# Products of an all-zero stationary operand added at five places of a four-layer attention kernel

## The chip, the cores and the metric

The program runs on 1 core of one Trainium2 chip. The metric is the device time of one execution in microseconds (us), lower is better. Before the change three executions took 2467.56, 2470.31 and 2482.42 us; the median is 2470.31 us.

## What is computed

An activation `x` of 2 x 1024 tokens with 288 features passes through four layers. The context has 2 x 154 rows of 288 features, and there are 16 heads of 18 features each.

Layers L0 and L1 have the same form. The quantised linear layer rounds activations and weights to 8-bit integers with scales of their own:

```python
h = layer_norm(x, ln1_g, ln1_b, 1e-06)
q8, s, sm = quant_act(h)
q, k, v = (quant_linear(q8, s, sm, w, b) for w, b in ((wq1, bq1), (wk1, bk1), (wv1, bv1)))
a = attn(q, k, v)                                   # self-attention, 1024 keys
x = x + quant_linear(*quant_act(a), wo1, bo1)
h = layer_norm(x, ln2_g, ln2_b, 1e-05)
q = quant_linear(*quant_act(h), wq2, bq2)
a = attn(q, cond @ wk2.T + bk2, cond @ wv2.T + bv2, mask)   # cross-attention, 154 keys
x = x + quant_linear(*quant_act(a), wo2, bo2)
h = quant_linear(*quant_act(layer_norm(x, ln3_g, ln3_b, 1e-05)), wfc1, bfc1)   # 1152 wide
x = x + quant_linear(*quant_act(gelu(h)), wfc2, bfc2)
```

Layers L2 and L3 are plain: `x` is projected to queries, attends in two separate softmaxes to the first 86 and to the last 68 context rows, and two output projections are added to `x`.

## The kernel before

Tokens lie on the 128 partitions; four blocks of 128 tokens make one row tile of 512. The code writes out a program order by hand, as Python generators that are advanced in turn (`beside`), and the framework then orders the instructions of each engine at build time on a timeline of its own (`schedule_with_timeline_sim=True`), taking what is ready and comes first in program order. On the chip each engine runs its own list in that order.

**Main stream.** `self_attention` makes 32 steps (2 layers x 2 batch elements x 4 head groups x 2 halves of the queries), `run` (L869) drives them. A step has `pre` (fetches by DMA on SP's queue), `maxima` of the next step (`self_maxima`: 32 products at L600 and 32 reductions on VectorE at L607, then `store_maxima`: parts on GpSimd, four transposes at L575, a copy on ScalarE at L581 and DMAs on ScalarE's queue at L585 into rows 108 to 119 of the next step's query tile), and `products` (`attend`, L695): for each of 8 key tiles four products of keys and queries (`weights_unit`, L660) with an Exp on ScalarE (L662), and, one key tile later, `weigh` (L701), which adds the four heads' weighted values into one PSUM tile `po` of pool `ps_o`, which has one buffer. The last `weigh` of a step (m = 7) is in `end`, which `run` calls after the first unit of the next step; `heads_back` then reads `po`.

**Side stream.** Beside the main stream run the weights' preparation (`prep_*`), the projections for the next self-attention (`SelfAttention.prepare`), and for each layer and batch element `cross_attention` (L1175) and `feed_forward` (L1312). In `cross_attention` the values of the context come from `context_values` (L1167, products at L456) once `wv` has been loaded on GpSimd's queue; `transpose_mask` (L1228) copies the last mask columns on ScalarE (L1232) and transposes eight blocks on TensorE (L1238). In `feed_forward`, `linear` (L1324) makes a 1152-wide row block with 12 products, `gelu` (L1336) runs two Gelu activations back to back on ScalarE (L1338, L1339), `integers` quantises, `output` transposes (L1354) and multiplies (L1360).

**Plain layers.** Layers L2 and L3 run as 8 blocks of 4 steps. `attend_pairs` (L822) makes eight key-query products a step (L660, Exp at L662), and `weigh` (L832) twice a step weighs two heads by two key spans into a new `po` of pool `ps_o` (L674), which VectorE transposes out (L847). `out` (L1494) makes the output projection.

PSUM tiles of the side stream, of the transposes and of the projections come from `mm` (L145), pool `ps_m` with two buffers used in turn. `zero16` of the change is the stationary operand, `ident16` the 128x128 identity in bf16 that is there already.

Of the kernel before, what the change touches and what calls it, by code (L numbers as in the profile page):

```python
# [11 lines left out]
BF16 = mybir.dt.bfloat16  # L12
# [4 lines left out]
P = 128  # L17
# [36 lines left out]
def tile_xattn(ctx: ExitStack, tc: tile.TileContext, ins: dict, out: bass.AP):  # L54
    nc = tc.nc
# [3 lines left out]
    const = ctx.enter_context(tc.tile_pool(name="const", bufs=1))  # L59
# [16 lines left out]
    nc.vector.memset(neghalf, -0.5)  # L76
    nmagic = const.tile([P, 1], F32, name="nmagic")
    nc.vector.memset(nmagic, -MAGIC)

# [66 lines left out]
    def mm(name, dtype=F32):  # L148
        n = 512 if dtype == F32 else 1024
        return ps_m.tile([P, n], dtype, tag="mm", name=name)  # L150
# [517 lines left out]
    def strips(po, pairs, start, stop):  # L668


        last = None
        for i in reversed(range(4)):
            lhsT, rhs = pairs[i]
            made = nc.tensor.matmul(  # L674
                po[32 * i : 32 * i + 32, :], lhsT=lhsT, rhs=rhs, start=start, stop=stop
            )
            if last is not None:
                follow(made, last)
            last = made
# [15 lines left out]
    def attend(qt, g, key_tiles, a, name):  # L695


        po = ps_o.tile([P, HQ], F32, tag="o", name=f"{name}o")
        made = {}

        def weigh(m):  # L701
            es, v = made.pop(m)
            strips(
                po,
                [(columns(v, 4 * g + j), es[j]) for j in range(4)],
                m == 0,
                m == len(key_tiles) - 1,
            )

        def step(m, half):  # L710
            keys, v = key_tiles[m]
            if half == 0:
                if m - 1 in made:
                    weigh(m - 1)
                made[m] = [], v
            for j in (2 * half, 2 * half + 1):
                made[m][0].append(weights_unit(qt, j, keys, P, f"{name}s"))

        def end():
            weigh(len(key_tiles) - 1)  # L720
            ptv, rec = heads_back(po, f"{name}o")
            av = a().rearrange("p c (g i d) -> p c g i d", g=G, i=4)
            nc.vector.tensor_tensor(
                av[:, :, g, :, :],
                ptv[:, :, :, 0:D],
                rec.unsqueeze(3).to_broadcast([P, HC, 4, D]),
                ALU.mult,
            )

        todo = [  # L730
            lambda m=m, half=half: step(m, half)
            for m in range(len(key_tiles))
            for half in range(2)
        ]
        return todo, end
# [86 lines left out]
    def attend_pairs(qt, g, keys, vs, features, name):  # L822

        made = {}

        def exps(j, n):
            k0, k1 = ((0, NTXT), (NTXT, T))[n]
            made[j, n] = weights_unit(
                qt, j, lambda j: keys(j)[:, k0:k1], k1 - k0, f"{name}s"
            )  # L830

        def weigh(j0):  # L832
            h0 = 4 * g + j0
            po = ps_o.tile([P, HQ], F32, tag="o", name=f"{name}o")
            strips(
                po,
                [
                    (columns(vs[n], h0 + j), made.pop((j0 + j, n)))
                    for j in range(2)
                    for n in range(2)  # L840
                ],
                True,
                True,
            )

            t = row512(f"{name}T")
            nc.vector.transpose(t, po)  # L847
            tv = t.rearrange("p (b e) -> p b e", e=32)
            rec = small.tile([P, HQ // 32, 1], F32, tag="rec", name=f"{name}rec")
            nc.vector.reciprocal(rec, tv[:, :, D : D + 1])  # L850
            features.add(tv, rec)

        def step(j0, n, j):
            if (j0, n, j) == (2, 0, 1):
                weigh(0)
            exps(j0 + j, n)

        todo = [
            lambda j0=j0, n=n, j=j: step(j0, n, j)
            for j0 in (0, 2)  # L860
            for n in range(2)
            for j in range(2)
        ]
        return todo, lambda: weigh(2)

    def nothing():
# [308 lines left out]
    def cross_attention(w, b, name):  # L1175
# [10 lines left out]
        wv = load_f32(bpool, w["pre"] + "wv2", 1)  # L1186
        v = bpool.tile([P, VW], F32, tag="v", name=f"{name}v")
        nc.gpsimd.memset(v, 1.0)
        context_values(v, P, b * T, wv, w["bv"], f"{name}cv")

        nr = T - P
# [36 lines left out]
        def transpose_mask(hf):  # L1228
            maskTs[hf] = bpool.tile([P, 2, HQ], F32, tag="maskT", name=f"{name}mT")

            others = view(row512(f"{name}mo"), c=HC, j=4, k=32)
            nc.scalar.copy(  # L1232
                others, masks[hf][:, :, P:TP].unsqueeze(2).to_broadcast([P, HC, 4, 32])
            )
            for kc in range(2):
                pt = mm(f"{name}mp")
                for c in range(HC):
                    nc.tensor.transpose(  # L1238
                        pt[:, c * P : (c + 1) * P],
                        others[:, c].rearrange("p j k -> p (j k)")  # L1240
                        if kc
                        else masks[hf][:, c, 0:P],
                        ident,
                    )
                nc.scalar.copy(maskTs[hf][:, kc, :], pt)
# [66 lines left out]
    def feed_forward(w, b, name):  # L1312

        qw2, row2 = w["2"]
        for hf in range(2):
            c0 = b * 8 + hf * HC
            s1 = small.tile([P, HC], F32, tag="st", name=f"{name}st")
            q = ln_quantise(c0, w["ln"], 1e-5, s1, f"{name}l")
            yield 8
            qT = transposed(q, f"{name}t")  # L1320
            yield 2
            hs, gs = {}, {}

            def linear(c):  # L1324
                hs[c] = big(f"{name}h")
                for j, wj in enumerate(w["1"]):
                    quant_linear(
                        qT,
                        c,
                        wj,  # L1330
                        s1[:, c : c + 1],
                        hs[c][:, j * C : (j + 1) * C],
                        f"{name}f",
                    )

            def gelu(c):  # L1336

                a = nc.scalar.activation(hs[c + 1], hs[c + 1], AF.Gelu)  # L1338
                follow(nc.scalar.activation(hs[c], hs[c], AF.Gelu), a)  # L1339

            def integers(c):
                s = small.tile([P, HC], F32, tag="s", name=f"{name}s")[:, 0:1]
                g = bf(f"{name}g")[:, 0:FZ]
                nc.gpsimd.memset(g[:, FF + NZ : FZ], 0.0)
                quantise(hs[c].unsqueeze(1), g.unsqueeze(1), s, 1, FF, f"{name}qs")
                gs[c] = g, s

            def output(c):
                g, s = gs[c]
                gT = view(bf(f"{name}gT")[:KF, 0 : 10 * P], k=10, t=P)  # L1350
                for k0 in (0, 5):
                    ptv = view(mm(f"{name}pt", BF16)[:KF, 0 : 5 * P], k=5, t=P)
                    for k in range(5):
                        nc.tensor.transpose(  # L1354
                            ptv[:, k, :], g[:, (k0 + k) * KF : (k0 + k + 1) * KF], ident16
                        )
                    nc.scalar.copy(gT[:, k0 : k0 + 5, :], ptv)  # L1357
                ps = mm(f"{name}o")[:, 0:C]
                for k in range(10):
                    nc.tensor.matmul(  # L1360
                        ps,
                        lhsT=gT[:, k, :],
                        rhs=qw2[:, k, :],
                        start=(k == 0),
                        stop=(k == 9),
                    )
                t = tmp(f"{name}u")
                nc.vector.scalar_tensor_tensor(t, ps, s, row2, ALU.mult, ALU.mult)
                add_to_x(c0 + c, t)


            for f, c in (
                (linear, 0),
                (linear, 1),
                (gelu, 0),
                (integers, 0),
                (linear, 2),
                (output, 0),
                (integers, 1),
                (linear, 3),  # L1380
                (gelu, 2),
                (output, 1),
                (integers, 2),
                (integers, 3),
                (output, 2),
                (output, 3),
            ):
                f(c)
                if f is not gelu:
                    yield 2  # L1390
# [357 lines left out]
```

## Time and profile before

| | |
|---|---|
| three runs, us | 2467.56, 2470.31, 2482.42 |
| span of the profiled execution, us | 2474.0 (a time of that execution beside its span is not given) |
| PE, matmuls | 1950.8 us busy, 79%, 10524 instructions |
| DVE | 1772.7 us, 72% |
| ACT | 1476.1 us, 60% |
| POOL | 972.2 us, 39% |
| mean granted TensorE clock | 0.866 of full speed |
| L660 128x512 products, self-attention | 1024, mean 409 ns |
| L674 weighing, self-attention | 2048 instructions (two for each f32 product), mean 660 ns |
| L1338 Gelu table load, Gelu | 16 of each line, 1283 and 1163 ns |

PE is TensorE's matmuls and transposes, PEld its weight loads, DVE VectorE, ACT ScalarE, POOL GpSimd, SP the engine that issues most DMAs. PEclk is the clock that TensorE was granted. Matmuls overlap in the pipeline, so the duration of one is longer than the distance between two. Idle time in brackets stands ahead of an instruction, with what ended it.

### The profile page before, as it was taken

To read this page: it belongs to the slowest core of one execution; us is meant where nothing else is said; L and a number is where in the kernel's file an instruction comes from. 1 tells how busy PE (TensorE), PEld (TensorE's weight loads), DVE (VectorE), ACT (ScalarE), POOL (GpSimd) and SP (SyncE) were. 2 spreads that over 40 slices of the span, in tenths; PEclk is the share of its full clock that TensorE was granted. 3 is DMA by queue.
4 is the path that set the end of the run, shared out by engine and by line. 5 is a ranking of instruction groups with operands and counts; after the bars stand their busy time and mean duration, and the time that the engine had idled before them with its cause. 6 is when DMAs were issued, how large, how long until landed. Compare 5 with 4: busy or idle time off the path is not lost. (4 is left out here: it accounts for less than half of the span.)

```text
span 2474.0 us, 33572 instructions
## 1 busy us (share of the span) xinstructions
PE 1950.8 (79%) x10524; PEld 847.7 (34%) x10524; DVE 1772.7 (72%) x4213; ACT 1476.1 (60%) x2897; POOL 972.2 (39%) x2038
## 2 busy tenths in 40 slices
PE   2579988788776878887679668887778886788887
PEld 1223333332233243323333233333334343443443
DVE  6699987699775658997559848893345686656665
ACT  3257767676477667756766257756646564554443
POOL 4334224651325455532353545523157462423210
PEclk9689999899787979998889589986877888889998
DMA  3523212221001322110032031100122311212221
GB/s 75 168 66 100 68 35 69 70 64 33 13 7 47 113 71 64 44 29 14 6 100 85 23 86 43 46 9 12 31 76 87 89 48 28 55 51 81 81 66 37
DMA packets 160003, 141.58 MB, mean 57 GB/s; under 512 B 44123, under 2 KB 156339, under 8 KB 159760
## 3 DMA queue, kind: packets, MB, share of 16 engines
q1 hardware_dynamic: 148656, 121.90, 17.0%
q0 software_dynamic: 3584, 12.04, 2.0%
q10 hardware_dynamic: 7584, 5.47, 1.2%
q8 instruction: 84, 1.38, 0.2%
q14 instruction: 95, 0.78, 0.1%
HBM read 96.60 MB, written 39.37 MB: 55 GB/s over the span
## 5 line engine op out<-in xcount | busy, mean ns | idle before, releaser
L662 ACT ACTIVATE L_xattn_aatse<-L_xattn_aats 128x512 f32<-128x512 f32 x1024 | 576.3, 597 | 277.1 <-PE L_xattn_aats L660 267.2
L607 DVE TENSOR_REDUCE L_xattn_amxh<-L_xattn_amx 128x1 f32<-128x512 f32 x1024 | 658.4, 679 | 74.5 <-PE L_xattn_amx L600 71.9
L660 PE MATMUL L_xattn_aats<-L_xattn_aqT,kT 120*128 120x512 bf16 x1024 | 392.2, 409 | 88.0 <-ACT L_xattn_aatse L662 46.2
L600 PE MATMUL L_xattn_amx<-kT,L_xattn_aqT 108*128 108x512 bf16 x1024 | 387.9, 414 | 65.1 <-DVE L_xattn_amxh L607 39.5
L674 PE MATMUL L_xattn_aato<-L_xattn_aatse,L_xattn_av 128*32 128x512 f32 x2048 | 300.9, 660 | 43.7 <-ACT L_xattn_aatse L662 40.6
L641 POOL TENSOR_TENSOR L_xattn_bmxm<-L_xattn_bmxm,L_xattn_bm 128x308 f32<-128x308 f32 x256 | 200.0, 787 | 158.4 <-ACT L_xattn_bmxm L640 150.4
L660 PEld LDWEIGHTS <-kT 120*128 120x128 bf16 x1024 | 96.7, 101 | 336.2 <-issue 298.7
L662 ACT ACTIVATE L_xattn_atse<-L_xattn_ats 86x512 f32<-86x512 f32 (+1 forms) x256 | 142.7, 590 | 95.0 <-PE L_xattn_ats L660 82.2
L600 PEld LDWEIGHTS <-L_xattn_aqT 108*128 108x128 bf16 x1024 | 102.7, 103 | 216.7 <-issue 162.5
L646 DVE TENSOR_REDUCE L_xattn_mxn<-L_xattn_mx 128x2 f32<-128x172 f32 (+1 forms) x512 | 124.8, 303 | 30.7 <-PE L_xattn_mx L630 27.4
L640 ACT COPY L_xattn_bmxm<-L_xattn_bmx 128x308 f32<-128x308 f32 x256 | 104.1, 417 | 67.9 <-PE L_xattn_bmx L630 23.7
L646 DVE TENSOR_REDUCE L_xattn_bmxn<-L_xattn_bmxm 128x2 f32<-128x308 f32 x256 | 116.8, 461 | 30.6 <-POOL L_xattn_bmxm L641 30.3
L660 PE MATMUL L_xattn_ats<-L_xattn_qT,L_xattn_kT 120*86 120x512 bf16 (+1 forms) x256 | 99.7, 422 | 40.8 <-DMA L_xattn_qT<-L_xattn_mxsr 18.6
L746 DVE TENSOR_TENSOR L_xattn_batse<-L_xattn_bats,L_xattn_bmT 128x512 f32<-128x512 f32 x160 | 107.5, 680 | 25.7 <-PE L_xattn_bats L752 7.5
L747 ACT ACTIVATE L_xattn_batse<-L_xattn_batse 128x512 f32<-128x512 f32 x160 | 100.3, 631 | 40.6 <-DVE L_xattn_batse L746 36.4
L1494 PE MATMUL L_xattn_o<-wo,L_xattn_p 128*128 128x288 f32 x320 | 99.9, 451 | 5.5 <-DVE L_xattn_p L819 4.6
L674 PEld LDWEIGHTS L_xattn_aato<-L_xattn_aatse,L_xattn_av 128*32 128x32 f32 x2048 | 42.2, 112 | 173.2 <-ACT L_xattn_aatse L662 144.1
L847 DVE STREAM_TRANSPOSE L_xattn_atT<-L_xattn_ato 128x512 f32<-128x512 f32 x64 | 45.6, 713 | 61.6 <-PE L_xattn_ato L674 50.1
L630 PE MATMUL L_xattn_mx<-L_xattn_kT,L_xattn_qT 108*128 108x154 bf16 x512 | 68.9, 250 | 24.1 <-DMA L_xattn_qT<-L_xattn_r 10.4
L630 PE MATMUL L_xattn_bmx<-L_xattn_bkT,L_xattn_bqT 108*128 108x154 bf16 x512 | 72.0, 244 | 16.1 <-ACT L_xattn_bmxm L640 7.1
L1360 PE MATMUL L_xattn_co<-L_xattn_wfc2t,L_xattn_cgT 117*128 117x288 bf16 x320 | 62.4, 346 | 23.4 <-ACT L_xattn_cgT L1357 22.4
L674 PE MATMUL L_xattn_ato<-L_xattn_atse,L_xattn_v 68*32 68x512 f32 (+1 forms) x512 | 74.9, 649 | 6.7 <-ACT L_xattn_atse L662 5.8
(632 smaller groups left out, 3782.0 us busy)
## 6 DMA issues: line engine op xcount, KB each, us to landing
kT<-L_xattn_akr SPq DMA_DIRECT2D x192, 72.0 KB
L_xattn_aqT<-L_xattn_aqr SPq DMA_DIRECT2D x192, 72.0 KB
L_xattn_bqT<-L_xattn_bqr SPq DMA_DIRECT2D x192, 72.0 KB
L_xattn_qT<-L_xattn_r SPq DMA_DIRECT2D x192, 72.0 KB
L_xattn_akr<-L_xattn_akst SPq DMA_DIRECT2D x16, 324.0 KB
L_xattn_aqr<-L_xattn_aqst SPq DMA_DIRECT2D x16, 324.0 KB
L_xattn_bqr<-L_xattn_bqst SPq DMA_DIRECT2D x16, 324.0 KB
L_xattn_r<-L_xattn_qst SPq DMA_DIRECT2D x16, 324.0 KB
```

The source lines that it names most:

```text
L600: nc.tensor.matmul(sp, lhsT=qt[:KR, j, c * P : (c + 1) * P], rhs=kt[:KR, j, a * 512 : (a + 1) * 512], start=True, stop=True,)
L607: nc.vector.tensor_reduce(halves[:, a, c, j, :], sp, AX.X, ALU.max, negate=True)
L630: nc.tensor.matmul(sp[:, j * T : (j + 1) * T], lhsT=qt[:KR, 2 * a + j, c * P : (c + 1) * P], rhs=kt[:KR, 4 * g + 2 * a + j, 0:T], start=Tr ...
L640: nc.scalar.copy(lm, of)
L641: nc.gpsimd.tensor_tensor(lm, lm, mask[:, c : c + 1, 0:T].to_broadcast([P, 2, T]), ALU.add)
L646: nc.vector.tensor_reduce(nm[:, c, 2 * a : 2 * a + 2, n], of[:, :, k0:k1], AX.X, ALU.max, negate=True,)
L660: nc.tensor.matmul(sp, lhsT=keys(j), rhs=qt[:KM, j, :], start=True, stop=True)
L662: nc.scalar.activation(e, sp, AF.Exp)
L674: made = nc.tensor.matmul(po[32 * i : 32 * i + 32, :], lhsT=lhsT, rhs=rhs, start=start, stop=stop)
L746: nc.vector.tensor_tensor(e, sp, maskT[:, m, :], ALU.add)
L747: nc.scalar.activation(e, e, AF.Exp)
L1494: nc.tensor.matmul(ps, lhsT=t[:, c * P : (c + 1) * P], rhs=wo[:, u0 + u, :], start=(u == 0), stop=(u == len(tiles) - 1),)
```

## The change

A 128x128 tile of zeros in bf16 is made once. A helper issues products of it (stationary) with the identity repeated four times (moving, 512 columns) into a PSUM tile. The products are issued at five places:

- `attend`, first unit of a step: 3 products that add zero to the still open `po` of the step before (31 of the 32 steps have one before).
- `attend_pairs`, `weigh`: 2 products into the new `po`, ahead of the weighing that overwrites it (64 calls).
- `cross_attention`, ahead of `context_values`: 6 products into a fresh `mm` tile (4 calls).
- `transpose_mask`, behind the copy on ScalarE: 6 products into a fresh `mm` tile (8 calls).
- `feed_forward`, behind the two Gelus: 9 products into a fresh `mm` tile (16 calls).

```diff
+    zero16 = const.tile([P, P], BF16, name="zero16")
+    nc.vector.memset(zero16, 0.0)
+    opened = []
+
+    def zeros(to, n, start):
+        for _ in range(n):
+            nc.tensor.matmul(
+                to,
+                lhsT=zero16,
+                rhs=ident16.unsqueeze(1).to_broadcast([P, 4, P]),
+                start=start,
+                stop=start,
+            )
+
+    def warm_open(n):
+        for po in opened[-1:]:
+            zeros(po, n, False)
+
+    def warm(n):
+        zeros(mm("warm"), n, True)
...
@@ attend, weigh
+            opened[:] = [po] if m < len(key_tiles) - 1 else []
@@ attend, step
             if half == 0:
+                if m == 0:
+                    warm_open(3)
                 if m - 1 in made:
@@ attend_pairs, weigh
             po = ps_o.tile([P, HQ], F32, tag="o", name=f"{name}o")
+            zeros(po, 2, True)
             strips(
@@ cross_attention
         nc.gpsimd.memset(v, 1.0)
+        warm(6)
         context_values(v, P, b * T, wv, w["bv"], f"{name}cv")
@@ transpose_mask
+            warm(6)
             for kc in range(2):
@@ gelu
                 follow(nc.scalar.activation(hs[c], hs[c], AF.Gelu), a)
+                warm(9)
```

## The prediction

> **What bounds the kernel now.** I read the page first, for engines and clock.
>
> ```profile
> span 2474.0 us, 33572 instructions
> PE 1950.8 (79%) x10524; PEld 847.7 (34%) x10524; DVE 1772.7 (72%) x4213; ACT 1476.1 (60%) x2897; POOL 972.2 (39%) x2038
> PEclk9689999899787979998889589986877888889998
> PE 10%; ACT 3%; DMA 3%; DVE 2%; issue 1%; SPq 1%; POOL 0%; ACTq 0%; DVEq 0%; POOLq 0%
> ```
>
> No engine is full. TensorE leads with 1950.8 us and is idle for 2474.0 - 1950.8 = 523 us. The last line is the chain that ended last: it could be followed through a fifth of the span only, and half of that fifth is PE. So a microsecond on PE is worth about half a microsecond of time, and the clock line says that PE's microseconds are dear: on average 0.866 of full speed was granted. Second, the windows view, cut on the grid on which the clock changes (3.413 us); behind each engine's busy time and count stand the clock (PEclk), the DMA engines' share and GB/s.
>
> ```profile
> core 0: us, PE busy (x) PEld busy (x) DVE busy (x) ACT busy (x) POOL busy (x), PEclk, DMA share, GB/s
> 1198.79:1202.20 3.41, 3.41 (x24) 1.63 (x24) 1.78 (x5) 2.17 (x5) 0.00 (x0) 1.00 0.02 5
> 1202.20:1205.62 3.42, 0.54 (x4) 0.19 (x2) 1.32 (x4) 3.39 (x4) 0.00 (x0) 1.00 0.00 0
> 1205.62:1209.03 3.41, 1.68 (x8) 0.20 (x8) 3.41 (x7) 1.67 (x2) 0.59 (x2) 0.50 0.00 0
> 1209.03:1212.44 3.41, 1.46 (x14) 1.12 (x10) 1.19 (x4) 2.16 (x4) 1.03 (x3) 0.50 0.00 0
> 1212.44:1215.86 3.42, 3.12 (x15) 1.94 (x14) 0.72 (x3) 3.39 (x7) 0.81 (x5) 0.50 0.02 5
> 1215.86:1219.27 3.41, 2.70 (x22) 1.63 (x21) 2.43 (x7) 1.80 (x4) 3.20 (x5) 1.00 0.00 0
> ```
>
> The clock is full or half, and the PE busy time of one window sets the next one. Counted over the 678 windows after the first 160 us: of full-speed windows under 0.6 busy 57 of 64 were followed by half speed, of those over 0.66 busy 1 of 413; of half-speed windows under 0.78 busy none of 70 was followed by full speed, of those over 0.88 busy 64 of 74. At half speed lie 174 windows, 594 us, with 467 us of PE work in them, in some 70 runs, mostly of 1 to 3 windows. Third, what makes such a hole (timeline, ScalarE, then TensorE):
>
> ```profile
> 1201.88 1.28 ACT L1338 ACT_TABLE_LOAD   x1
> 1203.17 1.16 ACT L1338 ACTIVATE L_xattn_ch<-L_xattn_ch 128x1152 f32<-128x1152 f32 x1
> 1204.24 1.15 ACT L1339 ACTIVATE L_xattn_ch<-L_xattn_ch 128x1152 f32<-128x1152 f32 x1
> 1205.40 1.28 ACT L662 ACT_TABLE_LOAD   x1
> ...
> 1207.35 1.94 PE L674 MATMUL L_xattn_aato<-L_xattn_aatse,L_xattn_av 128*32 128x512 f32 x8 [4.39 <-ACT L_xattn_aatse L662]
> ```
>
> Two Gelus with a table load on either side hold the Exps up for 4.9 us, TensorE stands still for 4.39 us, and the weighing behind it takes 1.94 us at half clock. The same eight instructions took 1.07 us at 1198.89.
>
> **The change part by part.** Nothing is removed. Added is one memset at the start (DVE, cover: PE has 3.5 us of work in the first 50 us), and 31 x 3 + 64 x 2 + 4 x 6 + 8 x 6 + 16 x 9 = 93 + 128 + 24 + 48 + 144 = 437 products of 512 bf16 columns. No DMA and no step moves. The nearest row is the 128x512 product of L660:
>
> ```profile
> 1200.86 0.60 PE L660 MATMUL L_xattn_aats<-L_xattn_aqT,kT 120*128 120x512 bf16 x2
> 1395.72 1.01 PE L660 MATMUL L_xattn_aats<-L_xattn_aqT,kT 120*128 120x512 bf16 x2 [3.18 <-DMA L_xattn_aqT<-L_xattn_amxsr]
> ```
>
> One takes 0.38 us at full clock and 0.58 at half, so the second adds 0.22 and 0.43 us. All 437 take 96 us at full and 188 us at half clock. What of it is hidden I read from the timeline, place by place, as the idle PE time between the point from which the zeros can run and the work that they precede, at the price of the clock there.
>
> *Gelus, 9 each (2.0 us).* They need no Gelu, only an `mm` buffer, so the order at build time can put them into the hole. In the 8 us behind the Gelu's start PE is idle 3.5 us or more at 14 of 16 places, and 0.5 us at two (2119 and 2164 us). Pushed out: 2 x 1.5 = 3 us.
>
> *Head of a step, 3 each (0.66 us).* They write the open `po`, so they stand between weighing 6 and weighing 7 of the step before, not in the long stall that often follows weighing 7. The idle time there is 0 to 0.53 us at 17 places and at least 0.65 us at 14; place by place 13 of 20.5 us find room, 7 us are pushed out. Behind them wait weighing 7 and, through `heads_back`, the step's end.
>
> *Plain values, 2 each (0.43 us).* They wait for VectorE to have read the last `po` (L847), as the weighing did; then PE mostly waits for an Exp:
>
> ```profile
> PEld L_xattn_aato L674 <- ACT L_xattn_aatse L662: 144.1, 175, 4.7
> PEld L_xattn_ato L674 <- ACT L_xattn_atse L662: 26.5, 32, 2.1
> PE L_xattn_bmp L1238 <- ACT L_xattn_bmo L1232: 10.9, 4, 3.9
> PE L_xattn_bcvp L456 <- DMA L_xattn_wv<-in_L_xattn_wv_dram: 10.8, 3, 6.1
> ```
>
> In 32 of 64 cases there is a wait, 26.5 us in all. With the half-clock places, 21 of 30 us fit and 9 us are pushed out; behind them stand the products of L660 and L630.
>
> *Mask transposes and context values, 6 each (1.3 us).* The context values wait for their weights (10.8 us at three of four places), which covers 24 zeros: nothing. Four of eight mask transposes lie where PE is idle under 0.4 us: 5.5 us pushed out.
>
> Pushed out in all: 3 + 7 + 9 + 5.5 = 24.5 us of PE. At PE's half share of the chain: 12 us later. The ends are 0 (each push lands in a wait of another engine) and 96 us (no zero finds its hole, since the order is made for other times than the chip's).
>
> *What the clock gives back.* A zero adds 0.22 / 3.41 = 0.06 to the share of a full-speed window and 0.13 at half speed. Adding them window by window, with the thresholds above and 0.55 of the PE time where a window turns fast, 174 half-speed windows become about 153. Around 1202, for instance, 0.54 + 2.0 + 0.66 us is 0.94 of a window: the clock holds for the next one, and the weighing takes 1.07 for 1.94 us. But then 1.46 us (0.43 of a window) follows without zeros, and the clock falls there anyway. So each place buys one window or two, not the whole run. Twenty-one windows at 467 / 174 = 2.7 us of PE work, half of it saved, make 28 us; behind a hole PE's work waits for itself alone, so I take 24 us of it. The ends are 0 (the clock does not count zeros as work) and 467 / 2 = 233 us (it never falls); I take the low side since by the same placing about nine tenths of the half-speed windows hold no zeros.
>
> Sum: 2474 + 12 - 24 = 2462. The profiled execution's span lies 3.7 us over the median of the runs shown, 2470.3, and inside their spread; against that median the forecast is 2458 us, 0.5% less.
>
> **A rule weighed.** The row is that 174 windows of 678, a quarter, ran at half clock. The Trainium skill, "TensorE: Matmul & The Clock Gate" (Part 1), says that for modelling, the warm-up penalty is under 1% of a typical kernel's span; by it the change could gain at most an estimated 25 us, and the sum would end near 2474. Its table of what matters asks only that PE have no idle gap over about 3 us, while here windows that were 0.4 to 0.6 busy lost the clock in 31 of 37 cases. By the rule only the Gelu holes count.
>
> **The rivals.** *More stays fast than I count* (2415 to 2445). Work behind a hole is a chain of PE and ScalarE, and if it runs at full clock it is done earlier and the next hole is shorter. If each of the 16 Gelu places saves its three half-speed windows (1.68 + 1.46 + 3.12 us halved, 3.1 us) and the 60 others of plain and cross-attention half a microsecond each, that is 50 + 30 - 12 pushed = 68 us at most; half of it gives 2436. For it: the runs at half clock are short, so many could close at once. Against it: the zeros stand in few of those windows.
>
> *The zeros stand in the way* (2495 to 2530), slower. PE takes its list in order, and the zeros come ahead of ready work: a zero that waits for an `mm` buffer or for `po` blocks products of L660 behind it. The pushed part is then not 24.5 but half of all, and at a mixed price of 0.3 us, 437 x 0.3 / 2 = 65 us, at full share: +65 - 24 = +41, 2511. It decides once over 50 us of PE time is pushed onto the path, twice what I count. For it: the order is made for times that may differ; the new order of every engine can lengthen stalls too: from weighing 6 to the next step's first product took 34 us at step 12 (611 us) and 23 us at step 20 (1085 us), for like work. Against it: 523 us of idle PE.
>
> *It does nothing to the clock.* Zero products may not count as activity. Then only the push stays: +12 to +25, 2482 to 2495.
>
> **How the numbers follow.** Forecast 0.36 (2446 to 2475), more stays fast 0.35, in the way 0.22, clock unmoved 0.07. The runs shown spread by 0.6%, so a measurement of this kernel can tell about 1% (25 us) from no change. Faster by over 1% is the first rival, 0.35; slower the second with a little of the third, 0.23; the rest 0.42. The range leaves out the far end of each rival: 2415 to 2505. With cases of both signs in it, the likeliest one's own range is 2446 to 2475.
>
> **What would show it.** Right: half-speed windows near 150, mean clock near 0.88, the window behind each Gelu pair at full speed, the wait of 4.39 us filled with nine products 0.22 us apart. Wrong: zeros with L674 or L660 waiting behind them; idle PE time unchanged while PE's busy time has grown by 90 us or more; clock at 0.866 or under; or half-speed runs gone where no zeros stand, which would make it the first rival.

## The result and the profile after

The changed kernel takes 2497.65 us (median of 7 executions, 2480.53 to 2506.07) against 2470.22 us (7 executions, 2463.86 to 2482.42) for the kernel before, measured together. The ratio is 1.0107, with a 95% interval of 1.0084 to 1.0131: the change makes the kernel 1.1% slower, some 26 us. The forecast of 2458 us lay on the wrong side. The time itself is that of the rival "The zeros stand in the way".

The first lines answer to the page's lines of before.

```profile
span 2498.0 us, 34438 instructions
PE 2003.0 (80%) x10961; PEld 876.7 (35%) x10961; DVE 1783.7 (71%) x4214; ACT 1480.0 (59%) x2897; POOL 965.7 (39%) x2038
PEclk9689999899797899988889689898978988989999
PE 1%; DVE 0%; ACT 0%; DMA 0%; issue 0%; ACTq 0%; SPq 0%; DVEq 0%
```

TensorE is busy 52.2 us more and idle 28 us less: 523 us of idle time became 2498.0 - 2003.0 = 495. Their difference, 24 us, is what the span grew by. The mean clock rose from 0.866 to 0.888. The chain of waits breaks off at once here (1%) and says nothing. The groups by line and shape show what the zeros took.

```profile
L86 PE MATMUL warm<-ident,zero 128*128 128x512 bf16 x216 | 52.9, 388 | 1.1 <-DVE L_xattn_ch L490 1.0
L86 PE MATMUL L_xattn_ato<-ident,zero 128*128 128x512 bf16 x128 | 40.0, 393 | 6.1 <-DVE L_xattn_atT L874 5.6
L86 PE MATMUL L_xattn_aato<-ident,zero 128*128 128x512 bf16 x93 | 27.2, 404 | 0.0
```

The figure behind the second bar is idle time ahead of the group: 1.1, 6.1 and 0.0 us. So at the heads and in the side stream the zeros begin almost without exception directly behind another product; at the plain values some begin behind a short wait for VectorE. In the pipeline nine of them take 2.11 us (see below), 0.38 for the first and 0.22 for each further one; 437 take an estimated 97 us of TensorE (added up from each start to the start of the next product it is 102 us). As the busy time grew by only 52 us, the other products took some 45 us less, at a clock that was higher on the mean. On the prediction's own count of the windows after 160 us, 489 us lie at half clock, 143 windows for 174.

What became of the hole behind the Gelus is seen on the timeline (start, duration, engine, line; idle time in brackets), ScalarE first, at about the place shown in the prediction. L697 and L683 are L674 and L660 of before.

```profile
1213.20 1.28 ACT L1367 ACT_TABLE_LOAD   x1
1214.49 1.16 ACT L1367 ACTIVATE L_xattn_ch<-L_xattn_ch 128x1152 f32<-128x1152 f32 x1
...
1212.11 0.53 PE L479 MATMUL L_xattn_cf<-L_xattn_wfc_864t,L_xattn_ctqT 100*128 100x288 bf16 x3
1212.48 2.11 PE L86 MATMUL warm<-ident,zero 128*128 128x512 bf16 x9
1214.42 0.60 PE L683 MATMUL L_xattn_aats<-L_xattn_aqT,kT 120*128 120x512 bf16 x2
1214.86 0.53 PE L479 MATMUL L_xattn_cf<-L_xattn_wfc_0t,L_xattn_ctqT 100*128 100x288 bf16 x3
1215.23 0.53 PE L479 MATMUL L_xattn_cf<-L_xattn_wfc_288t,L_xattn_ctqT 100*128 100x288 bf16 x3
1216.00 0.53 PE L479 MATMUL L_xattn_cf<-L_xattn_wfc_576t,L_xattn_ctqT 100*128 100x288 bf16 x3 [0.24 <-DVE L_xattn_ch L490]
1218.67 1.41 PE L697 MATMUL L_xattn_aato<-L_xattn_aatse,L_xattn_av 128*32 128x512 f32 x8 [2.14 <-ACT L_xattn_aatse L685]
```

The nine zeros start 2.0 us before the first Gelu, and products follow them without a gap. TensorE then still waits 2.14 us for the Exp. At 15 of the 16 places the zeros start 0.6 to 2.3 us ahead of the first Gelu, and behind none of the 16 groups does TensorE have idle time. The windows on the clock's grid tell the rest (columns as in the prediction).

```profile
core 0: us, PE busy (x) PEld busy (x) DVE busy (x) ACT busy (x) POOL busy (x), PEclk, DMA share, GB/s
1212.43:1215.85 3.42, 3.33 (x19) 1.68 (x18) 0.94 (x2) 3.39 (x5) 0.00 (x0) 1.00 0.00 0
1215.85:1219.26 3.41, 1.12 (x11) 0.35 (x10) 2.62 (x3) 3.23 (x4) 0.00 (x0) 1.00 0.00 0
1219.26:1222.67 3.41, 3.41 (x15) 1.01 (x8) 1.20 (x6) 0.91 (x2) 0.76 (x4) 0.50 0.00 0
```

The zeros lie in the first window; the hole's window is busy 1.12 of 3.41 us, and half speed follows it as before. At the head of a step it looks like this:

```profile
237.30 1.06 PE L697 MATMUL L_xattn_aato<-L_xattn_aatse,L_xattn_av 128*32 128x512 f32 x8
238.30 0.39 PE L683 MATMUL L_xattn_aats<-L_xattn_aqT,kT 120*128 120x512 bf16 x1
238.53 0.81 PE L86 MATMUL L_xattn_aato<-ident,zero 128*128 128x512 bf16 x3
239.18 0.38 PE L683 MATMUL L_xattn_aats<-L_xattn_aqT,kT 120*128 120x512 bf16 x1
...
241.20 1.07 PE L697 MATMUL L_xattn_aato<-L_xattn_aatse,L_xattn_av 128*32 128x512 f32 x8
```

The same two weighings before the change:

```profile
235.32 1.06 PE L674 MATMUL L_xattn_aato<-L_xattn_aatse,L_xattn_av 128*32 128x512 f32 x8
...
238.76 1.06 PE L674 MATMUL L_xattn_aato<-L_xattn_aatse,L_xattn_av 128*32 128x512 f32 x8
```

After the change come weighing 6 (237.30), one product, three zeros and the next product, with no gap. Weighing 7 (241.20) follows 3.90 us behind weighing 6; before the change it was 3.44 us here. All 31 groups at heads have work directly behind them.

### The profile page after: what moved, and what is told of

Read it like the earlier page. It is cut to its first block, busy times and chain, and to the rows that moved or that the text cites. A ratio compares the mean times of both kernels' runs of the same rounds, so it can differ in the third digit from the quotient of the medians.

```text
span 2498.0 us, 34438 instructions
## 1 busy us (share of the span) xinstructions
PE 2003.0 (80%) x10961; PEld 876.7 (35%) x10961; DVE 1783.7 (71%) x4214; ACT 1480.0 (59%) x2897; POOL 965.7 (39%) x2038
## 5 line engine op out<-in xcount | busy, mean ns | idle before, releaser
L683 PE MATMUL L_xattn_aats<-L_xattn_aqT,kT 120*128 120x512 bf16 x1024 | 394.6, 408 | 85.6 <-ACT L_xattn_aatse L685 40.7
L697 PE MATMUL L_xattn_aato<-L_xattn_aatse,L_xattn_av 128*32 128x512 f32 x2048 | 286.8, 633 | 35.6 <-ACT L_xattn_aatse L685 32.2
L683 PEld LDWEIGHTS <-kT 120*128 120x128 bf16 x1024 | 98.9, 102 | 324.5 <-issue 282.8
L683 PE MATMUL L_xattn_ats<-L_xattn_qT,L_xattn_kT 120*86 120x512 bf16 (+1 forms) x256 | 94.8, 410 | 24.0 <-DMA L_xattn_qT<-L_xattn_mxsr 11.7
L697 PEld LDWEIGHTS L_xattn_aato<-L_xattn_aatse,L_xattn_av 128*32 128x32 f32 x2048 | 41.4, 110 | 161.4 <-ACT L_xattn_aatse L685 133.2
L1524 PE MATMUL L_xattn_o<-wo,L_xattn_p 128*128 128x288 f32 x320 | 94.9, 435 | 3.6 <-DVE L_xattn_p L845 3.2
L236 POOL CAST L_xattn_mxst<-L_xattn_mxn 128x32 bf16<-128x32 f32 x32 | 8.0, 251 | 187.8 <-DVE L_xattn_mxn L669 133.6
L697 PE MATMUL L_xattn_ato<-L_xattn_atse,L_xattn_v 68*32 68x512 f32 (+1 forms) x512 | 71.2, 630 | 8.0 <-ACT L_xattn_atse L685 7.2
```

What stands on the lines that cost most here:

```text
L683: nc.tensor.matmul(sp, lhsT=keys(j), rhs=qt[:KM, j, :], start=True, stop=True)
L697: made = nc.tensor.matmul(po[32 * i : 32 * i + 32, :], lhsT=lhsT, rhs=rhs, start=start, stop=stop)
L1524: nc.tensor.matmul(ps, lhsT=t[:, c * P : (c + 1) * P], rhs=wo[:, u0 + u, :], start=(u == 0), stop=(u == len(tiles) - 1),)
```

## The experiments

Two theories were set against each other. **Theory 1, the pushed products:** the zeros are issued as soon as a PSUM buffer allows, ahead of products that are ready, and cost TensorE time on the path. **Theory 2, the order:** 437 further instructions make the planner order every engine's list anew, and the new order is worse. Every ratio is against the kernel before on the same chip, with its 95% interval; single executions of one kernel differ by some 0.4% either way, so spans are used only where they show where time went. "Old order" means that every engine's other instructions keep the sequence that they had before the change, by ordering edges between neighbours in one engine's list, which add no wait. The edits are shown shortened.

### One place alone

**e1_only_heads** (93 products), in the order that the planner then chooses:

```diff
-            zeros(po, 2, True)
-        warm(6)
-            warm(6)
-                warm(9)
```

> Only the 3 zero products at the head of a step (93 in all, 20.5 us of PE at 0.22 us each). Theory 1, products pushed onto the path: they stand between the weighing of key tile 6 and that of key tile 7, where PE has little idle time, so the self-attention steps get longer by 0.5 to 0.7 us each: +10 to +20 us. Theory 2, the new order of all engines costs and not the products themselves: the difference has no relation to the number of products, anywhere between -10 and +25 us, and the steps without side work (2 to 5) stay as they were.

Measured: 1.0025 (1.0004 to 1.0046), some 6 us: below theory 1's range and inside the wide one of theory 2.

**e2_only_plain** (128 products):

```diff
-                    warm_open(3)
+                    pass
-        warm(6)
-            warm(6)
-                warm(9)
```

> Only the 2 zero products ahead of the plain values (128 in all, 28 us of PE). Theory 1: the plain stage has TensorE as its busiest engine, so half or more of it is pushed out: +8 to +20 us, all of it after 1830 us of the span. Theory 2: differences already before 1830 us, or a total outside of that range.

Measured: 1.0072 (1.0050 to 1.0094), some 18 us, inside theory 1's range.

**e3_only_context_mask** (72 products):

```diff
-                    warm_open(3)
+                    pass
-            zeros(po, 2, True)
-                warm(9)
```

> Only the 6 zero products ahead of the context values and of the mask transposes (72 in all, 16 us of PE). Theory 1: 0 to +8 us. Theory 2: anything from -15 to +15 us, since the order of the four cross-attentions changes with it.

Measured: 0.9977 (0.9959 to 0.9995), some 6 us faster: outside theory 1's range and inside theory 2's.

**e4_only_gelu** (144 products):

```diff
-                    warm_open(3)
+                    pass
-            zeros(po, 2, True)
-        warm(6)
-            warm(6)
```

> Only the 9 zero products behind the Gelus (144 in all, 32 us of PE). Theory 1: they lie in the hole of 4 us that two Gelus and two table loads leave, and one to two windows of clock are won at each of 16 places: -15 to 0 us. Theory 2: a difference of more than 5 us to the slower side although the hole is filled.

Measured: 1.0055 (1.0037 to 1.0073). The Gelu products, which I had taken to lie in the hole, lose time by themselves; that part of theory 1 as I had it fell, and the time is what was named for theory 2. The four add up to 0.25 + 0.72 - 0.23 + 0.55 = 1.29%, against 1.07% together. Each of these kernels has an order of its own, so these numbers do not yet tell the theories apart.

### Order and products, each without the other

**e5_order_alone**: all zeros gone, every engine's list kept as the changed kernel has it.

```diff
-            zeros(po, 2, True)
...
+    for queue in sorted(ORDER):      # ORDER: the list of each engine, after the change
+        for k0, k1 in zip(places, places[1:]):
+            tc.add_manual_dep(traced[k1], traced[k0].name, NoSync, reason="given order")
```

> No zero products at all, but every engine's instructions in the order that they have in the changed kernel (given by edges that fix the order and add no wait). Theory 1, the products themselves cost: no difference, -5 to +5 us. Theory 2, the new order costs: +15 to +35 us, most of the change's 26 us without a single added product.

Measured: 1.0146 (1.0122 to 1.0169), 36 us. Theory 1's "no difference" fell, and what was expected of theory 2 came, at the upper end of its range. The new order without its zeros is, if anything, slower than with them (1.0107, 1.0084 to 1.0131; the two intervals just overlap).

```profile
span 2509.7 us, 33582 instructions
PE 1969.6 (78%) x10524; PEld 860.1 (34%) x10524; DVE 1781.5 (71%) x4213; ACT 1476.6 (59%) x2897; POOL 964.8 (38%) x2038
```

The same products as before take 18.8 us more of TensorE (1969.6 for 1950.8), and 17 us more are idle (540 for 523). The mean clock of its four executions was 0.859 to 0.863, against 0.863 to 0.879 in those of the kernel before beside them. At half clock lie 631 us, for 594 before. So about half of what this order loses goes with a lower clock.

**e6_zeros_old_order**: all 437 products, the other instructions in the old order.

```diff
+            zero_names.add(z.ins.name)   # left out of the ordered list
...
+    for queue in sorted(ORDER):      # ORDER: the list of each engine, before the change
+        for k0, k1 in zip(places, places[1:]):
+            tc.add_manual_dep(traced[k1], traced[k0].name, NoSync, reason="given order")
```

> All 437 zero products, but the other instructions of every engine in the order that they had before the change (given by edges). Theory 1: +15 to +35 us, as the change. Theory 2: the products in themselves cost little or gain, -15 to +8 us.

Measured: 1.0119 (1.0093 to 1.0145). With the order held, the loss is that of the change, 29 us for 26, as expected of theory 1. So the zeros cost without any new order (e6), and the new order costs without any zeros (e5). The two do not add: 1.19% and 1.46% alone, 1.07% together. Either is enough for a loss of this size, and the share of each in the changed kernel cannot be told from these runs.

```profile
span 2496.3 us, 34438 instructions
PE 1997.9 (80%) x10961; PEld 873.8 (35%) x10961; DVE 1780.5 (71%) x4214; ACT 1480.1 (59%) x2897; POOL 974.3 (39%) x2038
```

**e16_before_pinned**: the kernel before with the same edges, to price them.

```diff
+    for queue in sorted(ORDER):      # before.py and its own lists
+        for k0, k1 in zip(places, places[1:]):
+            tc.add_manual_dep(traced[k1], traced[k0].name, NoSync, reason="given order")
```

> The kernel before with its own order given by the edges. Control: the edges leave each engine's list as it was, so -4 to +4 us. If giving the order costs by itself, +10 us or more, and the runs in the old order would have to be read against it.

Measured: 1.0001 (0.9982 to 1.0021). The edges cost nothing that can be measured, so e6 and the runs below can be read as they stand.

Where the time goes was sought in the key-query products of the plain layers, one line each from before, after, e5 and e6 (after the count: shortest, median and longest ns, first and last start in us).

```profile
L660 PE MATMUL L_xattn_ats<-L_xattn_qT,L_xattn_kT x256: 376/380/655, 1851.2 to 2457.2; 120*86 120x512 bf16 x64, 120*68 120x512 bf16 x64
```

```profile
L683 PE MATMUL L_xattn_ats<-L_xattn_qT,L_xattn_kT x256: 376/379/652, 1858.8 to 2482.4; 120*86 120x512 bf16 x64, 120*68 120x512 bf16 x64
```

```profile
L705 PE MATMUL L_xattn_ats<-L_xattn_qT,L_xattn_kT x256: 375/380/656, 1863.9 to 2494.1; 120*86 120x512 bf16 x64, 120*68 120x512 bf16 x64
```

```profile
L729 PE MATMUL L_xattn_ats<-L_xattn_qT,L_xattn_kT x256: 376/380/655, 1871.0 to 2481.8; 120*86 120x512 bf16 x64, 120*68 120x512 bf16 x64
```

From first to last they take 606.0 us before, 623.6 after, 630.2 in the new order without zeros and 610.8 with zeros in the old order. Taken alone this would put most of the new order's loss into the plain layers. But the same stretch in the old order, without a full-size product of zeros in it, takes 606.0, 611.1, 619.8 and 624.5 us (before, e10, e16 and e13; e10 has short ones there, e13 has its zeros at the heads alone), so one profile each cannot show that. The first start can show more: it is 1842 to 1856 us where no or hardly any full-size zeros lie ahead of it (before, e8, e10, e16) and 1871 us in e6, so at least 15 us of what the zeros lose in the old order lie ahead of the plain layers. Where the new order loses its time stays open.

### One place alone in the old order

The edit is that of e6 with the calls of e4, e2, e3 and e1. **e7_gelu_old_order**:

```diff
+    for queue in sorted(ORDER): ...      # as e6
-                    warm_open(3)
-            zeros(po, 2, True)
-        warm(6)
-            warm(6)
```

> The 9 zero products behind the Gelus alone, in the old order of all else. Theory 1 (products cost): +14 us as without the fixed order. Theory 2 (the order costs): these products lie in the 4 us hole, so -10 to +3 us.

Measured: 1.0056 (1.0036 to 1.0076), the same as in a free order (1.0055). Theory 2 fell for the Gelu place. Its timeline, TensorE and then ScalarE:

```profile
1206.08 0.53 PE L525 MATMUL L_xattn_cf<-L_xattn_wfc_864t,L_xattn_ctqT 100*128 100x288 bf16 x3
1206.45 2.11 PE L131 MATMUL warm<-ident,zero 128*128 128x512 bf16 x9
1208.39 0.53 PE L525 MATMUL L_xattn_cf<-L_xattn_wfc_0t,L_xattn_ctqT 100*128 100x288 bf16 x3
...
1215.26 1.91 PE L743 MATMUL L_xattn_aato<-L_xattn_aatse,L_xattn_av 128*32 128x512 f32 x8 [4.39 <-ACT L_xattn_aatse L731]
...
1209.78 1.28 ACT L1410 ACT_TABLE_LOAD   x1
```

And the two products of the linear layer between which the zeros stand, in the kernel before (L456 there):

```profile
1200.12 0.53 PE L456 MATMUL L_xattn_cf<-L_xattn_wfc_864t,L_xattn_ctqT 100*128 100x288 bf16 x3
1200.49 0.53 PE L456 MATMUL L_xattn_cf<-L_xattn_wfc_0t,L_xattn_ctqT 100*128 100x288 bf16 x3
```

Before, the second followed the first after 0.37 us; here the zeros stand between them and it comes 2.31 us later. The nine zeros run 3.3 us ahead of the table load, and the hole is the same 4.39 us that the prediction showed, with the weighing behind it still at half clock (1.91 us).

**e8_plain_old_order**:

```diff
+    for queue in sorted(ORDER): ...      # as e6
-                    warm_open(3)
-        warm(6)
-            warm(6)
-                warm(9)
```

> The 2 zero products ahead of the plain values alone, in the old order of all else. Theory 1: +18 us as without the fixed order. Theory 2: under +8 us; TensorE is the busiest engine of this stage, so some of the 28 us may still be pushed out.

Measured: 1.0023 (1.0003 to 1.0042), where the free order gave 1.0072. Two thirds of the plain place's loss in the free order came with the order.

**e12_context_mask_old_order**:

```diff
+    for queue in sorted(ORDER): ...      # as e6
-                    warm_open(3)
-            zeros(po, 2, True)
-                warm(9)
```

> The 6 products ahead of the context values and of the mask transposes alone, in the old order of all else. Theory 1: these 12 groups stand ahead of waits on a DMA or on a copy, 16 us of TensorE of which a third is pushed out: -8 to +5 us. Theory 2 (the 0.2% gained without the fixed order came from a lucky order): 0 to +8 us.

Measured: 1.0017 (0.9992 to 1.0042). The products themselves show no gain here; that of e3 then came with its order, though the two intervals touch.

**e13_heads_old_order**:

```diff
+    for queue in sorted(ORDER): ...      # as e6
-            zeros(po, 2, True)
-        warm(6)
-            warm(6)
-                warm(9)
```

> The 3 products at the head of a step alone (93), in the old order of all else. If the four places add up in the old order (plain 0.23%, Gelu 0.56%, context and masks 0.17%, all together 1.19%), the heads are left with 0.2%: +2 to +10 us. If they do not add up (one place's products spoil or help another's), outside of that.

Measured: 1.0038 (1.0018 to 1.0058). In the old order the places add up: 0.56 + 0.23 + 0.17 + 0.38 = 1.34%, against 1.19% for all in e6, within the intervals. Each place alone loses or shows nothing.

### What in the products costs the time

**e10_short_old_order**: all 437, in the old order, with 16 columns instead of 512.

```diff
-                to,
+                to[:, 0:16],
-                rhs=ident16.unsqueeze(1).to_broadcast([P, 4, P]),
+                rhs=ident16[:, 0:16],
```

> All 437 products at their places, in the old order of all else, but of 16 columns and not 512: a thirtieth of the streaming, no weight on the clock. Theory 1 (their TensorE time costs): -4 to +8 us. A rival that their mere presence costs (weight loads, PSUM buffers taken, waits for them): +15 to +30 us, as with 512 columns.

Measured: 1.0005 (0.9983 to 1.0027). The instructions, their weight loads and their buffers, held for 16 columns, cost nothing that can be measured; the columns do.

**e14_double_old_order**: 874 products of 512 columns, in the old order.

```diff
-        for _ in range(n):
+        for _ in range(2 * n):
```

> Twice the number of products at each place (874), in the old order of all else. If each product costs the TensorE time that it takes and the clock has given back what it can, the second 437 cost more than the first, 94 us of TensorE at a share of a half or more: +65 to +110 us against before. If the cost is in the places and not in the number, +25 to +40 us; if the clock gains more with more products, under +25 us.

Measured: 1.0385 (1.0359 to 1.0410), some 95 us, in the first range. The first 437 cost 29 us, the second 66.

```profile
span 2567.5 us, 35316 instructions
PE 2073.5 (81%) x11398; PEld 904.5 (35%) x11398; DVE 1780.8 (69%) x4214; ACT 1481.2 (58%) x2897; POOL 973.0 (38%) x2038
```

TensorE's idle time is 2567.5 - 2073.5 = 494 us. It went from 523 us without zeros to 498 with 437 (e6, 2496.3 - 1997.9) and then stayed. In these executions idle time fell by 25 us with the first half of the zeros and by hardly any with the second. The time at half clock, on the same count, fell from 594 to 476 and then to 419 us: there the return fell too.

**e11_identity**: the changed kernel, with the identity as the stationary operand at the 344 products that write a tile afresh.

```diff
-                lhsT=zero16,
+                lhsT=ident16 if start else zero16,
```

> The changed kernel, with the identity as the stationary operand and not zeros at the four places whose product is overwritten or never read (344 of 437); same order, same sizes. If products of zeros count as activity like others, the time (2498 us) and the clock (0.89) stay within 0.4%; if the clock does not count zeros in full, the clock rises by 0.01 or more and the time falls by 10 us or more.

Measured: 1.0116 (1.0084 to 1.0147), mean clock 0.887 to 0.896 over its executions, against 0.888 to 0.904 for the changed kernel: no difference that can be told. The identity is itself mostly zeros, but the windows of the changed kernel settle it: 22 windows at full speed were over 0.66 busy and would have been under 0.6 without their zeros, and all 22 were followed by full speed, where before the change 57 of 64 windows under 0.6 were followed by half speed. So the clock counts products of zeros as work.

### The zeros at another instant

**e9_gelu_wait**: only the Gelu place; the nine products wait for the first of the two Gelus, so they cannot run ahead of the hole; free order.

```diff
-                warm(9)
+                warm(9, a)
...
+                tc.add_manual_dep(z.ins, behind.ins.name, Sync, reason="behind the Gelu")
```

> The 9 products behind the Gelus alone, but made to wait for the first Gelu of the pair, so that they cannot stand ahead of it. Theory 1 (the products cost where they stand ahead of work that is ready, and the hole behind the Gelu is free): -12 to +3 us instead of the +14 us of the products that need not wait. Theory 2 (the new order of the rest costs): +8 to +20 us still, since the order of all engines differs from before here too.

Measured: 1.0025 (1.0003 to 1.0048), some 6 us, between the ranges of the two theories: half of the 0.55% is gone.

**e15_order_of_gelu_wait**: the order of e9 without any zeros, as e5 is to the change.

```diff
+    for queue in sorted(ORDER): ...      # as e5, with the lists of e9
-                warm(9, a)
```

> No product of zeros, but the order of the kernel whose products behind the Gelus wait for the first Gelu. If the products in the hole gain something in their own order, this is slower than that kernel's +0.25%: +10 to +20 us. If they gain nothing and cost a little, it is at -5 to +5 us.

Measured: 1.0072 (1.0049 to 1.0095). Against their own order the zeros of e9 gain: 1.0025 / 1.0072 = 0.9953. The same quotient for the whole change is 1.0107 / 1.0146 = 0.9962.

**e17_gelu_hole_old_order**: the nine products wait for the first Gelu and are written ahead of `output`, and all else keeps the old order.

```diff
+                behind[c] = a
-                warm(9)
...
+                if c in behind:          # in output(c)
+                    warm(9, behind[c])
```

> The 9 products behind the Gelus alone, made to wait for the first Gelu, traced at the head of the output step so that their PSUM buffer fits the old order, and the old order of all else. If products that fill the hole gain and the order was what spoiled it in the kernel that waits (+0.25% with them, +0.72% for its order without them): -20 to -5 us, faster than both kernels. If they do nothing when nothing else moves: -4 to +4 us. If they cost here too: +5 us or more.

Measured: 0.9969 (0.9949 to 0.9988), 7.7 us faster than before and the lowest ratio of the study (the interval of e3 overlaps it). TensorE, at about the place shown before (L752 and L1419 are L674 and L1338 of before; this profiled execution took 2479.91 us, longer than the median of 2470.11 us):

```profile
1199.77 0.53 PE L534 MATMUL L_xattn_cf<-L_xattn_wfc_864t,L_xattn_ctqT 100*128 100x288 bf16 x3 [0.21 <-DVE L_xattn_ch L545]
1201.74 3.28 PE L131 MATMUL warm<-ident,zero 128*128 128x512 bf16 x9 [1.44 <-ACT L_xattn_ch L1419]
1204.94 1.54 PE L752 MATMUL L_xattn_aato<-L_xattn_aatse,L_xattn_av 128*32 128x512 f32 x8
1208.44 0.77 PE L1438 MATMUL L_xattn_cpt<-ident,L_xattn_cg 128*117 128x128 bf16 x10 [1.96 <-ACT L_xattn_cg L467]
```

At this place the picture is the one that I had predicted: TensorE waits 1.44 us for the Gelu, the zeros fill the rest of the hole, and the weighing follows without a gap. It is not so everywhere: at seven of the 16 places the zeros come directly behind the first Gelu, at nine later, 3.0 to 9.3 us behind its start. Over all 16 places the idle time of TensorE in the 8 us behind the first Gelu's start is 64.7 us before, 59.7 us in e7 and 40.7 us in e17. So the 144 zeros, 31 us at full clock, took up 5 us of that idle time without the wait, and 24 us with it. The windows:

```profile
1199.12:1202.53 3.41, 1.75 (x11) 0.79 (x10) 1.46 (x3) 3.38 (x4) 0.00 (x0) 1.00 0.00 0
1202.53:1205.95 3.42, 3.42 (x15) 0.79 (x12) 3.19 (x7) 2.08 (x3) 0.19 (x1) 0.50 0.00 0
1205.95:1209.36 3.41, 1.30 (x18) 0.63 (x10) 1.61 (x4) 2.17 (x4) 1.43 (x3) 1.00 0.00 0
```

The 1.44 us ahead of the zeros still cost one window (1.75 busy, then half speed), but that window is full, and the next one is at full speed again. On the same count 522 us lie at half clock in e17, 573 us in e7 and 594 us before. Between e7 and e17 the same 144 products moved by a few microseconds, and the time by 0.87% of the kernel.

**e18_gelu_hole_five**: as e17 with five products.

```diff
-                    warm(9, behind[c])
+                    warm(5, behind[c])
```

> As the run before, with 5 products and not 9 (1.1 us of the hole and not 1.9 us). If the gain comes from keeping the window over the clock's threshold, 5 hold it less often: -10 to 0 us. If the products' own time is what counts, 5 are better than 9 by 5 us or more.

Measured: 0.9990 (0.9971 to 1.0010), not to be told from no change, nor from the nine products of e17. Other counts, and waits of the same kind at the other four places, were not tried.

## Why the prediction was wrong

**The bound was read rightly.** TensorE at a clock that falls is what the time hangs on: once the idle time fell no further, 75.6 us more of TensorE's busy time made the span 71 us longer (e14 against e6).

**The price of a product was right.** 0.22 us each at full clock; 437 take some 97 to 102 us, for 96 forecast.

**The step that failed: "so the order at build time can put them into the hole".** I read from the timeline how much idle time lies somewhat behind each point from which the zeros can run, and took it for filled. The zeros do not go where the idle time is. They need only a buffer or the open `po`, come earlier in program order than the work behind them, and run ahead of it; the hole opens later and stays (2.14 us in after, 4.39 us in e7). From that came the mis-sized term, the 24.5 us pushed out. By the two profiles idle time took up only 28 of 97 us, net of all else that changed, which leaves 69 us, above the 50 us from which I let the rival decide. The Gelu place, which I gave 3 us, lost 0.56%, 14 us net, alone in the old order: only 5 us of the idle time behind the Gelus went away, for 31 us of zeros. e17 shows the cause by turning it round: where the products must wait for the Gelu, 24 us of it go away, and the same 144 gain.

**A term was put at nothing: the order.** "No DMA and no step moves" holds for what the code asks for, but the planner ordered every engine's list anew, and my sum had no term for it. That order alone measured +1.46%, 36 us (e5). I had named it only within a rival.

**Half a share was wrong as well.** I multiplied by PE's half of a chain that covered a fifth of the span. That 69 us less the 45 us that the other products save give the 24 us by which the span grew follows from the span being busy plus idle time, and does not show the share. e14 does: of the second 437, an estimated 94 us of products, 66 us came out as time, and what did not was mostly won back by the clock.

**The clock gave back more than I took.** 31 windows fewer at half clock for 21, and 45 us of TensorE time for 24. With the order held it is the same: e6 has 594 - 476 = 118 us less at half clock, and the other products take 94 - 47 = 47 us less. The Trainium skill, "TensorE: Matmul & The Clock Gate" (Part 1), puts the ramp penalty, that of the first few microseconds of matmuls, at under 1% of a typical kernel's span. I had taken it as a limit for all time at half clock, which it does not claim to be: what the zeros won back here is an estimated 45 / 2474 = 1.8%.

**The rivals.** "The zeros stand in the way" came, in time and by its first mechanism as far as the place of the zeros shows it. Its second, that the new order costs, exists too: 1.46% in e5. Each alone makes the kernel as slow as the change does, and within the new order the zeros even seem to take about 0.4% back; which of the two makes the changed kernel slow is therefore not shown. "It does nothing to the clock" is out (0.888, and the windows under e11). "More stays fast" had its direction right for the clock and missed what the products cost.

**The signs that I named.** Half-speed windows near 150 (143) and a clock near 0.88 came, and so did not tell the forecast from the rival. The two others of being right, the filled wait and the full-speed window behind each Gelu pair, did not come where I showed the place; one of being wrong did, zeros with L660 directly behind them (L683 above).

**What stays open:** what in the new order costs its 36 us, beyond the lower clock, and why that cost and the zeros' own do not add up in the changed kernel.

## What to carry to other kernels

Work that is to fill a hole needs a dependence on what opens the hole; without one it ran here ahead of other work, and most of the hole stayed. Idle time near an instruction is room for it only if the list of that engine puts it there, so read what stands directly in front and behind, not how much is idle around. Where an edit makes a planner order everything anew, measure the edit with the old order held and the new order without the edit, before a cause is named.

## What the runs showed of the hardware that was not expected

Full-size products of zeros count for the clock (22 of 22 windows, under e11), while 437 of 16 columns left it at 0.867 to 0.878 for 0.864 to 0.876 before, and cost nothing that can be measured (e10: 1.0005). Doubling the zeros to an estimated 189 us of TensorE still left 419 us at half clock, for 594 without any (e14, mean clock 0.905): of the 122 windows at half clock that remain, 114 hold no zeros and follow no window that does. The clock does not need a long hole to fall: of the 68 falls from full to half speed in the kernel before, 52 came behind a window that no idle gap of over 3 us touched.
